# A two-layer decoder on one core: a fourth buffer for negated scores, half of the tails' sum and some elementwise work on Pool, the diagonals' product in one piece, reciprocals early

## The chip, the core and the metric

The kernel runs on one core of a Trainium2 chip, in one launch. The core has five engines, each with its own instruction stream that is executed in order: PE (TensorE, matmuls and transposes), DVE (VectorE), ACT (ScalarE), POOL (GpSimd) and SP (SyncE, which issues nearly all DMAs here). They wait for each other through semaphores. The metric is the device time of one execution in microseconds (us); lower is better. A time given for a kernel is the median of its runs.

## The reference, cut to what matters

Eight sequences (B = 8) of S = 256 tokens and width D = 256, 16 heads of 16, all in float32. Six sublayers follow each other, each with a residual and a LayerNorm without weights:

```python
x = norm(x + recurrence(x))                       # layer 0: gated linear scan
x = norm(x + cross(x, ctx, mask, side_bias))      # 16-head attention over ctx
x = norm(x + ternary_linear(quant(norm_gb(x))))   # one scale over all of x
x = norm(x + self_attention(x, rel_k, rel_v))     # layer 1: relative positions, clipped at 20
x = norm(x + cross(x, ctx, mask))                 # 16-head attention over ctx
x = norm(x + down(silu(gate(x)) * up(x)))         # hidden width 768
```

In the self-attention a score gets `q . rel_k[clip(j - i, -20, 20) + 20]` added, and the output gets `sum_j p[i, j] * rel_v[clip(j - i, -20, 20) + 20]`: 39 diagonals near the main one have a vector each, and all that lies further left or further right (the two tails) shares one vector a side. The quantisation scale of the ternary layer is a maximum over all eight sequences, so layer 1 can start for none of them before layer 0 is done for all.

## The kernel before, in words

**An order written out by a planner.** The kernel is generated by a small list scheduler (`Order`). Every piece of work is a Python generator that yields operations: `do(engine, cost, ready, emit)` for one engine, `either(ready, way, way)` where two engines could do it, `dma(...)` for SP. The planner holds a time at which each engine is free, and repeatedly takes the operation that can start first by its own cost figures (ties within 0.1 us go to the smaller urgency number, then to the earlier end), emits its instructions, and moves that engine's time on. So the order of every engine's stream is fixed when the program is built, and the costs in the source (`0.66`, `1.7`) are the planner's beliefs, not times of the chip. `copy` (L289 to L293) is such an `either` between DVE and ACT; it takes every transposed block of probabilities out of PSUM.

**Buffers are slots.** `get(slots, ...)` or a `Held` waits in the plan until a slot is free. PSUM has 8 banks. A quad of four heads takes four at once, each transposed block one, each attention item one for its output `pv` from its first `values` to the multiplication at L1041.

**An attention item** is one sequence in one of the three attentions (24 items). It projects q, k and v, then runs four quads (NS = 4) of four heads:
- `quad` (L896): the scores on PE (L913); for each head a DVE instruction pair at L941 that adds the bias, mask or band, negates, and takes the row minimum; its result `sn` is one of three `s_bufs` (L268), each held until ACT has read it.
- `head` (L952): two ACT exponentials (L957) which also sum the rows; four PE transposes of p (L502) and a copy to SBUF (L291 on DVE, L292 on ACT).
- `values` (L980): sixteen PE instructions at L995 that add into `pv`.
- `attend_out` (L1015), started after the last `values`: a reciprocal of the row sums on DVE (L1020), spread over 512 columns by POOL (L1026), transposed by PE, copied into `oT`, multiplied with `pv` (L1041), projected (L1056), added to x plus its bias row (L1049 on POOL, L1061 on DVE) and normalised.

**Self-attention has more.** The band of relative scores goes through DRAM by DMA and comes back skewed. After each quad, `tails_task` (L1377) sends p's diagonals to DRAM, masks the two tails with two POOL instructions (L1401, L1406: each 4 heads by 108 columns) and sums them with one DVE reduction over 864 elements (L1417). After each second quad two DMAs (L1425) bring the 39 diagonals into `acc`. `by_distance` (L1443), called by `attend_out`, then takes four rounds (two halves c by two blocks of tokens t), one after the other: four transposes of `acc` (L1455), a copy into one of two `at_bufs`, eight PE instructions at L1468 that add the product with `drv` into `pv`.

**A normalisation** (`norm`, L527) is statistics on DVE, the root on POOL (L543, L548), and a subtract-and-multiply on DVE (L553, two instructions of 256 columns; two pairs after the first cross-attention, which makes two normalised results).

**Other lines that the change touches.** L374 and L378 issue the first loads in the order bias columns, x of sequence 0, three weights. L1137 and L1585 turn a mask into 0 or a large negative number, on DVE. L1712 is the low half of a hidden activation (`sg - h`), on DVE, 24 times. `rows` (L407) holds bias rows for the whole kernel; `w0` is a pool of buffers that is given up when layer 0 is done.

Of the kernel before, what the change touches and what calls it, by code (L numbers as in the profile page):

```python
# [19 lines left out]
P = 128  # L20
# [202 lines left out]
def kernel(  # L223
# [43 lines left out]
    pts_bufs = slots(work, "pts", 8, [P, NQ, S])  # L267
    s_bufs = slots(work, "s", 3, [P, NQ, S])  # L268
    q_bufs = slots(work, "q", 3, [P, KC, S])
# [97 lines left out]
    def loads():  # L367
# [5 lines left out]

        t = yield from dma([0.0], 18432, lambda: nc.sync.dma_start(out=cols, in_=cols_in))  # L374
        yield from load_xT(0)
        for i in range(3):
            events["wa", i] = yield from dma(
                [0.0], 262144, lambda: nc.sync.dma_start(out=wa[i], in_=chunked(a_w[i]))  # L378
            )
        for b in range(1, 4):  # L380
            yield from load_xT(b)
        for a in range(3):
            pool = w0 if a == 0 else wts
            for i in range(2):
# [21 lines left out]
                )  # L406
                rows[o] = const.tile([P, D], F32, tag=f"rows{o}", name=f"rows{o}")  # L407
                events["rows", o] = yield from dma(
# [118 lines left out]
    def norm(y, t_y, make, name, make2=None):  # L527
# [21 lines left out]

        def scaled(make, i):  # L550
            dst = make()
            for t in range(NQ):
                nc.vector.tensor_scalar(  # L553
                    dst[:, t, :], y[:, t, :], mv[:, t, 0:1], rstd[:, i, t : t + 1], ALU.subtract,
                    ALU.mult,
                )

        t = yield from do("DVE", 0.9, [t_y], stats)
        t_r = yield from do("POOL", 0.9 if n == 1 else 1.1, [t], root)
        if n == 2:  # L560
            t_2 = yield from do("DVE", 0.66, [t_r], lambda: scaled(make2, 1))
        t = yield from do("DVE", 0.66, [t_r], lambda: scaled(make, 0))
        return t if n == 1 else (t, t_2)
# [388 lines left out]
    def head(it, n, j, p, s, nm, t, left, times):  # L952
# [165 lines left out]
    def item_x0(b):  # L1118
# [3 lines left out]
        if b > 1:  # L1122
# [134 lines left out]
    def layer1_self():  # L1257
        rel = layer1s.enter_context(tc.tile_pool(name="rel", bufs=1))
        kr_bufs = slots(rel, "kr", 2, [P, KC, 2, S - BW])
        wide_bufs = slots(rel, "wide", 2, [P, HH, PBW])  # L1260
        acc_bufs = slots(rel, "acc", 2, [P, KC, NQ, HH, NA])
        tail_bufs = slots(rel, "tail", 1, [P, NQ, 4, P - MR])
        at_bufs = slots(rel, "at", 2, [P, 4, P])
# [22 lines left out]
    def item_s1(b, kr_bufs, wide_bufs, acc_bufs, tail_bufs, at_bufs, band_bufs):  # L1286
# [90 lines left out]
        def tails_task(n, p, left, t_p):  # L1377
# [37 lines left out]
            t = yield from do(  # L1415
                "DVE", 1.0, [t],
                lambda: nc.vector.tensor_reduce(acc[:, c, :, own, 1], tail.tile, AX.X, ALU.add),  # L1417
            )
            tail.drop(t)
            it.t_tail.append(t)  # L1420
            if len(it.t_pb) in (2, 4) and n % 2 == 1:
                for g in range(P // BLK):
# [19 lines left out]

        def by_distance(t_pv):  # L1443
            for c in range(KC):
                t_a = yield from event(it.key("acc", c))
                for n in (2 * c, 2 * c + 1):
                    t_t = yield from event(it.key("tail", n))
                    t_a = max(t_a, t_t)
                for t in range(NQ):
                    ps = Held(banks, f"psa{b}_{t}_{c}")  # L1450
                    turned = lambda: ps.tile.rearrange("p a (j q) -> p (a j) q", q=P)

                    def emit():
                        for j in range(4):
                            nc.tensor.transpose(  # L1455
                                turned()[: 2 * NA, j, :],
                                it.acc.tile[:, c, t, 2 * j : 2 * j + 2, :].rearrange("p h r -> p (h r)"),
                                ident,
                            )

                    t_t = yield from do("PE", TURNS, [t_a, ps], emit)
                    at = yield from get(at_bufs, f"at{b}_{t}_{c}", t_t)
                    t_t = yield from copy([t_t, at.at], at.tile[: 2 * NA], turned()[: 2 * NA])
                    ps.drop(t_t)

                    def emit():
                        for j in range(4):
                            nc.tensor.matmul(  # L1468
                                it.pv.tile[32 * j : 32 * j + 32, c, t * P : (t + 1) * P],
                                drv[:, t, :],  # L1470
                                at.tile[: 2 * NA, j, :],
                                start=False,
                                stop=(t == NQ - 1 and c == KC - 1),
                                tile_position=(0, 32 * j),
                                skip_group_check=True,
                            )

                    t_pv = yield from do("PE", on_pe(256), [t_t, t_pv], emit, "v")
                    at.drop(t_pv)
            it.acc.drop(t_pv)  # L1480
            return t_pv

        it.by_distance = by_distance

# [83 lines left out]
    def item_x1(b):  # L1568
# [3 lines left out]
        if b > 0:  # L1572
# [84 lines left out]
    def gated(b, gu, dn, t_w, hT_bufs):  # L1657
# [13 lines left out]
        for i in range(NH // 2):  # L1671
            psg = Held(banks, f"fg{b}_{i}")

            def emit(ps, w):
# [34 lines left out]
            )  # L1709
            t = yield from do(  # L1710
                "DVE", on_dve(512), [t],
                lambda: nc.vector.tensor_tensor(h[:, 1], sg.tile, h[:, 0], ALU.subtract),  # L1712
            )
# [134 lines left out]
```

## Time and profile before

| | us |
|---|---|
| median of 3 runs (817.36 to 820.14) | 819.33 |
| the profiled execution | 817.66 |
| its span, first to last instruction | 815.9 |
| layer 0's recurrence and start, about | 0 to 75 |
| first cross-attention, about | 75 to 275 |
| ternary layer, then the first self-attention items alone | 275 to 380 |
| self- and cross-attention items in turn | 380 to 700 |
| feed-forward, with the last cross-attention items | 700 to 816 |

The stages overlap, so their borders are only where most of the work changes. The busy time of an engine is the time in which it had at least one instruction under way. PE's instructions are pipelined: the recorded duration of one is its latency, and the next one begins before it has ended. The granted PE clock was 0.995 of full speed over the span. What bounds the kernel is read from the lines that the prediction shows.

### The profile page before, as it was taken

To read this page: it belongs to the slowest core of one execution; us is meant where nothing else is said; L and a number is where in the kernel's file an instruction comes from. 1 tells how busy PE (TensorE), PEld (TensorE's weight loads), DVE (VectorE), ACT (ScalarE), POOL (GpSimd) and SP (SyncE) were. 2 spreads that over 40 slices of the span, in tenths; PEclk is the share of its full clock that TensorE was granted. 3 is DMA by queue.
4 is the path that set the end of the run, shared out by engine and by line. 5 is a ranking of instruction groups with operands and counts; after the bars stand their busy time and mean duration, and the time that the engine had idled before them with its cause. 6 is when DMAs were issued, how large, how long until landed. Compare 5 with 4: busy or idle time off the path is not lost.

```text
span 815.9 us, 21213 instructions
## 1 busy us (share of the span) xinstructions
PE 782.6 (96%) x7175; PEld 598.8 (73%) x7175; DVE 700.7 (86%) x2452; ACT 635.4 (78%) x2047; POOL 209.9 (26%) x398
## 2 busy tenths in 40 slices
PE   7999999999999999999999999999999999999995
PEld 6886777776777786656666777776777766799884
DVE  3899889988888698787899799899898998989985
ACT  2349988989988458896789799899899898846841
POOL 3520221121211044234333213242243322110020
PEclk9999999999999999999999999999999999999997
DMA  5735521100100449899976406645357443000001
GB/s 181 224 114 84 70 46 44 39 16 27 41 27 28 155 101 216 165 170 185 173 158 137 112 26 133 133 93 120 88 112 155 108 100 100 19 28 14 15 14 39
DMA packets 177681, 77.67 MB, mean 95 GB/s; under 512 B 155046, under 2 KB 171430, under 8 KB 177574
## 3 DMA queue, kind: packets, MB, share of 16 engines
q1 hardware_dynamic: 177574, 76.32, 41.9%
q8 instruction: 57, 0.93, 0.5%
q14 instruction: 50, 0.41, 0.2%
HBM read 41.66 MB, written 34.64 MB: 94 GB/s over the span
## 4 chain that ended last, share of the span: by engine, by line
PE 62%; DVE 13%; ACT 10%; DMA 6%; issue 4%; POOL 2%; SPq 2%; POOLq 0%; DVEq 0%; ACTq 0%
PE pt L502 14%; PE s L913 9%; PE pv L995 8%; ACT p L957 7%; PE pso L519 4%; DVE sn L941 4%; PE psv L519 4%; PE psq L508 4%; PE psk L508 3%; PE psd L1723 3%; ACT pts L292 2%; PE psa L1455 2%; DMA sk<-w 1%; PE fg L1678 1%; PE psr L1308 1%
## 5 line engine op out<-in xcount | busy, mean ns | idle before, releaser
L957 ACT ACTIVATE p<-sn,nm 128x256 f32<-128x256 f32 x768 | 381.3, 507 | 23.9 <-DVE nm L941 18.4
L502 PE MATMUL pt<-ident,p 128*128 128x128 f32 x1536 | 207.1, 277 | 5.2 <-ACT p L957 2.1
L502 PEld LDWEIGHTS pt<-ident,p 128*128 128x128 f32 x1536 | 169.4, 140 | 47.3 <-ACT p L957 24.7
L292 ACT COPY pts<-pt 128x512 f32<-128x512 f32 x274 | 147.7, 586 | 20.7 <-PE pt L502 19.8
L957 ACT ACTIVATION_READ_ACCUMULATOR p<-sn,nm 128x1 f32 x768 | 151.6, 197 | 0.0
L913 PE MATMUL s<-k,q 32*128 32x256 f32 (+2 forms) x1792 | 122.2, 371 | 2.6 <-DVE nm L941 1.2
L995 PE MATMUL pv<-pts,v 128*32 128x256 f32 x1536 | 107.4, 385 | 0.6 <-ACT pts L292 0.5
L941 DVE CUSTOM_DVE_ANT_0 sn<-s,band 128x256 f32<-128x256 f32 x256 | 93.9, 417 | 14.1 <-ACT p L957 6.3
L941 DVE CUSTOM_DVE_ANT_0 sn<-s,bias 128x256 f32<-128x256 f32 x256 | 93.8, 418 | 12.6 <-PE s L913 7.1
L941 DVE CUSTOM_DVE_ANT_0 sn<-s,hide 128x256 f32<-128x256 f32 x256 | 93.2, 417 | 12.9 <-PE s L913 10.6
L913 PEld LDWEIGHTS s<-k,q 32*128 32x128 f32 x1792 | 78.5, 184 | 34.2 <-issue 21.5
L291 DVE COPY pts<-pt 128x512 f32<-128x512 f32 x110 | 73.9, 683 | 4.5 <-PE pt L502 3.5
L995 PEld LDWEIGHTS pv<-pts,v 128*32 128x32 f32 x1536 | 42.9, 109 | 43.9 <-issue 19.8
L941 DVE DVE_READ_ACCUMULATOR2_ANT nm<- 128x1 f32 x768 | 62.8, 82 | 0.0
L519 PE MATMUL pso<-wvo,oT 128*128 128x256 f32 x192 | 47.1, 388 | 1.5 <-DVE oT L1041 1.5
L1026 POOL COPY rsw<-rsum 128x512 f32<-128x512 f32 x24 | 14.6, 610 | 126.2 <-DVE rsum L1020 99.0
L519 PEld LDWEIGHTS pso<-wvo,oT 128*128 128x128 f32 x192 | 34.8, 190 | 11.1 <-issue 3.2
L1318 POOL COPY w<-w 128x504 f32<-128x504 f32 x32 | 19.3, 603 | 87.8 <-DVE w L291 47.2
L1417 DVE TENSOR_REDUCE acc<-tail 128x8 f32<-128x864 f32 x32 | 33.4, 1043 | 3.0 <-POOL tail L1406 3.0
L1345 POOL COPY band<-ends 64x256 f32<-64x256 f32 x64 | 21.4, 360 | 47.1 <-DVE nm L941 47.0
L519 PE MATMUL psv<-wvo,ctxT 128*128 128x256 f32 x128 | 30.5, 381 | 0.3 <-DVE xnT L1093 0.3
L508 PE MATMUL psk<-ctxT,wqk 128*128 128x256 f32 x128 | 30.4, 381 | 0.0
(197 smaller groups left out, 1310.2 us busy)
## 6 DMA issues: line engine op xcount, KB each, us to landing
sk<-w SPq DMA_DIRECT2D x32, 416.0 KB
band<-sk SPq DMA_DIRECT2D x64, 104.0 KB
pb<-p SPq DMA_DIRECT2D x64, 104.0 KB
band<-sk SPq DMA_DIRECT2D x64, 84.0 KB
pb<-p SPq DMA_DIRECT2D x64, 84.0 KB
acc<-pb SPq DMA_DIRECT2D x32, 156.0 KB
ctxT<-in_ctxT SPq DMA_DIRECT2D x16, 256.0 KB
wpad<-in_qk_w SPq DMA_DIRECT2D x6, 512.0 KB
```

The lines of the kernel that those rows point to most:

```text
L291: ("DVE", on_dve(n), lambda: nc.vector.tensor_copy(dst, src)),
L292: ("ACT", on_act(n), lambda: nc.scalar.copy(dst, src)),
L502: nc.tensor.transpose(ps[:, c, t * P : (t + 1) * P], src[:, t, c * P : (c + 1) * P], ident)
L508: nc.tensor.matmul(ps, w[:, c, lo:hi], rhs[:, c, :], start=(c == 0), stop=(c == KC - 1))
L519: nc.tensor.matmul(ps[:, t, :], srcT[:, c, t * P : (t + 1) * P], w[:, c, :], start=(c == 0), stop=(c == KC - 1),)
L913: nc.tensor.matmul(ps[j].tile[:, t, first : first + w], it.q.tile[32 * j : 32 * j + 32, c, t * P : (t + 1) * P], k[32 * j : 32 * j + 32, c ...
L941: nc.vector.tensor_tensor_reduce(out=s.tile[:, t, :], in0=ps[j].tile[:, t, :], in1=tile[:, t, :], scale=-1.0, scalar=3e38, op0=ALU.add, op ...
L957: nc.scalar.activation(p.tile[:, j, q, :], s.tile[:, q, :], AF.Exp, bias=nm[:, q : q + 1], scale=-1.0, accum_out=it.sum_of(q, h),)
L995: nc.tensor.matmul(it.pv.tile[32 * j : 32 * j + 32, c, :], it.v.tile[:, k, head_of(n, j), :], pts.tile[:, k, :], start=(k == 0 and i == 0 ...
L1345: nc.gpsimd.tensor_copy(band.tile[0:BLK, :, t, lo:hi], it.ends[c][0:BLK, t, i:HH:2].unsqueeze(2).to_broadcast([BLK, 4, hi - lo]),)
L1417: lambda: nc.vector.tensor_reduce(acc[:, c, :, own, 1], tail.tile, AX.X, ALU.add),
L1723: nc.tensor.matmul(ps.tile[:, t, :], hT.tile[:, r, m, t * P : (t + 1) * P], dn[:, m, :], start=(m == 0 and r == 0), stop=(m == NH - 1 and ...
```

## The change

The list of what it does:
- `s_bufs` has four buffers instead of three. The bias rows of the first attention move from the pool that lasts for the whole kernel into `w0`.
- The first loads are issued in the order x of sequence 0, first weight, bias columns, other weights.
- In `norm`, the scaling of all but the recurrence's normalisation may run on DVE (planner's cost 0.66) or on POOL (1.7), whichever the planner finds free first.
- The low half at L1712 may run on DVE or on POOL (1.3).
- The two mask instructions (L1137, L1585) run on POOL.
- In `tails_task`, POOL adds the upper 54 columns of each masked tail to the lower 54, and the DVE reduction reads 432 elements instead of 864.
- The first part of `attend_out` (reciprocal, spreading, transposes, copy into `oT`) becomes a task of its own, `scales`, which starts when the last exponential's row sum is there, not after the last `values`.
- `by_distance` becomes `distances(c)`, a task that starts when the diagonals of the first half have been asked for; for each half it makes both blocks' transposes and copies, and then all sixteen PE instructions of the product in one piece, after the `values` of that half.

```diff
@@
-    s_bufs = slots(work, "s", 3, [P, NQ, S])
+    s_bufs = slots(work, "s", 4, [P, NQ, S])
@@ def loads():
-        t = yield from dma([0.0], 18432, lambda: nc.sync.dma_start(out=cols, in_=cols_in))
         yield from load_xT(0)
         for i in range(3):
             events["wa", i] = yield from dma(
                 [0.0], 262144, lambda: nc.sync.dma_start(out=wa[i], in_=chunked(a_w[i]))
             )
+            if i == 0:
+                yield from dma([0.0], 18432, lambda: nc.sync.dma_start(out=cols, in_=cols_in))
...
-                rows[o] = const.tile([P, D], F32, tag=f"rows{o}", name=f"rows{o}")
+                rows[o] = (w0 if a == 0 else const).tile([P, D], F32, tag=f"rows{o}", name=f"rows{o}")
@@ def norm(y, t_y, make, name, make2=None):
-        def scaled(make, i):
-            dst = make()
+        def scaled(engine, dst, i):
             for t in range(NQ):
-                nc.vector.tensor_scalar(
+                engine.tensor_scalar(
                     dst[:, t, :], y[:, t, :], mv[:, t, 0:1], rstd[:, i, t : t + 1], ALU.subtract,
                     ALU.mult,
                 )
+
+        def both(t, dst, i):
+            if name.startswith("l0a"):
+                return do("DVE", 0.66, [t], lambda: scaled(nc.vector, dst, i))
+            return either(
+                [t],
+                ("DVE", 0.66, lambda: scaled(nc.vector, dst, i)),
+                ("POOL", 1.7, lambda: scaled(nc.gpsimd, dst, i)),
+            )
...
-            t_2 = yield from do("DVE", 0.66, [t_r], lambda: scaled(make2, 1))
-        t = yield from do("DVE", 0.66, [t_r], lambda: scaled(make, 0))
+            t_2 = yield from both(t_r, make2(), 1)
+        t = yield from both(t_r, make(), 0)
@@ def head(it, n, j, p, s, nm, t, left, times):
         it.t_sums.append(t_e)
+        if len(it.t_sums) == H:
+            order.spawn(urgency(it, NS - 1), scales(it))
@@
-    def attend_out(it, t_pv):
-
-        ai, b = it.ai, it.b
+    def scales(it):
+
         rs = small.tile([P, NQ, H], F32, tag="rsum", name=f"rsum{it.name}")
...
-        oT = yield from get(oT_bufs, f"oT{it.name}", t)
+        oT = it.oT = yield from get(oT_bufs, f"oT{it.name}", t)
         t = yield from copy([t, oT.at], oT.tile, ps.tile)
         ps.drop(t)
+        events[it.key("scales")] = t
+
+    def attend_out(it, t_pv):
+
+        ai, b = it.ai, it.b
+        t = yield from event(it.key("scales"))
+        oT = it.oT
         if ai == 1:
-            t_pv = yield from it.by_distance(t_pv)
+            t_pv = yield from event(it.key("distances"))
@@ def item_x0(b):
-            "DVE", on_dve(512), [t_m, neg.at],
-            lambda: nc.vector.tensor_scalar(
+            "POOL", 0.6, [t_m, neg.at],
+            lambda: nc.gpsimd.tensor_scalar(
@@ def item_x1(b):
-            "DVE", on_dve(512), [t_m, hide.at],
-            lambda: nc.vector.tensor_scalar(
+            "POOL", 0.6, [t_m, hide.at],
+            lambda: nc.gpsimd.tensor_scalar(
@@ def tails_task(n, p, left, t_p):
+                for w in (54,):
+                    nc.gpsimd.tensor_tensor(
+                        tail.tile[:, :, :, 0:w], tail.tile[:, :, :, 0:w], tail.tile[:, :, :, w : 2 * w],
+                        ALU.add,
+                    )
+
-            t = yield from do("POOL", 1.06, [t_p, tail.at], emit)
+            t = yield from do("POOL", 2.1, [t_p, tail.at], emit)
...
-                "DVE", 1.0, [t],
-                lambda: nc.vector.tensor_reduce(acc[:, c, :, own, 1], tail.tile, AX.X, ALU.add),
+                "DVE", 0.55, [t],
+                lambda: nc.vector.tensor_reduce(
+                    acc[:, c, :, own, 1], tail.tile[:, :, :, 0:54], AX.X, ALU.add
+                ),
...
                 events[it.key("acc", c)] = t_d
+                if c == 0:
+                    order.spawn(urgency(it, NS - 1), distances(0))
@@
-        def by_distance(t_pv):
...
+        def distances(c):
+
+            t_a = yield from event(it.key("acc", c))
+            for n in (2 * c, 2 * c + 1):
+                t_t = yield from event(it.key("tail", n))
+                t_a = max(t_a, t_t)
+            at = yield from get(at_bufs, f"at{b}_{c}", t_a)
+            times = []
+            for t in range(NQ):
...
+                t_t = yield from do("PE", TURNS, [t_a, ps], emit)
+                t_t = yield from copy([t_t, at.at], at.tile[: 2 * NA, t], turned()[: 2 * NA])
+                ps.drop(t_t)
+                times.append(t_t)
+            t_v = yield from event(it.key("values", 2 * c + 1))
...
+            t_v = yield from do("PE", on_pe(512), [t_v, *times], emit, "v")
+            at.drop(t_v)
+            if c + 1 < KC:
+                yield from distances(c + 1)
+                return
+            it.acc.drop(t_v)
+            events[it.key("distances")] = t_v
@@ def gated(b, gu, dn, t_w, hT_bufs):
-            t = yield from do(
-                "DVE", on_dve(512), [t],
-                lambda: nc.vector.tensor_tensor(h[:, 1], sg.tile, h[:, 0], ALU.subtract),
+            t = yield from either(
+                [t],
+                ("DVE", on_dve(512), lambda: nc.vector.tensor_tensor(h[:, 1], sg.tile, h[:, 0], ALU.subtract)),
+                ("POOL", 1.3, lambda: nc.gpsimd.tensor_tensor(h[:, 1], sg.tile, h[:, 0], ALU.subtract)),
             )
```

More of the change, by code (lines that the diff above doesn't have):

```diff
@@ L1262, in layer1_self @@
         tail_bufs = slots(rel, "tail", 1, [P, NQ, 4, P - MR])
-        at_bufs = slots(rel, "at", 2, [P, 4, P])
+        at_bufs = slots(rel, "at", 1, [P, NQ, 4, P])
         bands = []
@@ L1441, in item_s1 @@
         it.t_pb = []
-        def by_distance(t_pv):
[L1444 to L1448, printed above, removed]
-                for t in range(NQ):
[L1450 to L1481, printed above, removed]
@@ L1483, in item_s1, with emit @@
-        it.by_distance = by_distance
+        def distances(c):
[6 more added lines that the diff above has]
+            for t in range(NQ):
+                ps = Held(banks, f"psa{b}_{t}_{c}")
+                turned = lambda: ps.tile.rearrange("p a (j q) -> p (a j) q", q=P)
+                def emit():
+                    for j in range(4):
+                        nc.tensor.transpose(
+                            turned()[: 2 * NA, j, :],
+                            it.acc.tile[:, c, t, 2 * j : 2 * j + 2, :].rearrange("p h r -> p (h r)"),
+                            ident,
+                        )
+                t_t = yield from do("PE", TURNS, [t_a, ps], emit)
[3 more added lines that the diff above has]
+            t_v = yield from event(it.key("values", 2 * c + 1))
+            def emit():
+                for t in range(NQ):
+                    for j in range(4):
+                        nc.tensor.matmul(
+                            it.pv.tile[32 * j : 32 * j + 32, c, t * P : (t + 1) * P],
+                            drv[:, t, :],
+                            at.tile[: 2 * NA, t, j, :],
+                            start=False,
+                            stop=(t == NQ - 1 and c == KC - 1),
+                            tile_position=(0, 32 * j),
+                            skip_group_check=True,
+                        )
+            t_v = yield from do("PE", on_pe(512), [t_v, *times], emit, "v")
[5 more added lines that the diff above has]
+            events[it.key("distances")] = t_v
```

## The prediction, made before the change was run

> **What bounds the kernel now.** I begin with the first part of the page and with the windows by stage (columns: length, then busy us of PE, its weight loads, DVE, ACT and POOL, clock, DMA share, GB/s).
>
> ```profile
> PE 782.6 (96%) x7175; PEld 598.8 (73%) x7175; DVE 700.7 (86%) x2452; ACT 635.4 (78%) x2047; POOL 209.9 (26%) x398
> ```
>
> ```profile
> 200.00:250.00 50.00, 49.56 (x470) 37.23 (x467) 43.95 (x179) 44.89 (x157) 9.06 (x12) 1.00 0.09 28
> 350.00:400.00 50.00, 47.15 (x463) 32.36 (x461) 39.71 (x139) 37.51 (x122) 19.38 (x42) 1.00 0.92 182
> 600.00:650.00 50.00, 49.62 (x521) 36.95 (x522) 44.38 (x172) 47.33 (x163) 15.92 (x33) 1.00 0.61 133
> 700.00:750.00 50.00, 49.81 (x434) 46.05 (x432) 44.16 (x105) 28.06 (x70) 5.42 (x10) 1.00 0.04 13
> ```
>
> PE looks full. If it were, no more than 815.9 - 782.6 = 33 us could be won. The Trainium skill (Trainium Kernel Development and Optimization, section Performance Expectations) says that matmul busy time is a bad measure because matmuls are pipelined, and names weight-load busy time instead: 73%. So I count PE's content from the timeline (start, length, what, how many):
>
> ```profile
> 524.21 1.89 PE L519 MATMUL psv<-wvo,xT_l0f 128*128 128x256 f32 x8
> 526.27 1.05 PE L995 MATMUL pv<-pts,v 128*32 128x256 f32 x16
> 530.15 2.78 PE L502 MATMUL pt<-ident,p 128*128 128x128 f32 x24
> ```
>
> One transpose is 277 ns long (its group's mean), but they follow each other by (2.78 - 0.28) / 23 = 0.109 us; a 256-column matmul by (1.89 - 0.38) / 7 = 0.216; a block of 16 counts between 0.67 (last start) and 1.05, I take 0.86. 1952 transposes 213 us, 960 projections 207, 192 blocks 165, feed-forward 576 x 0.12 (48 psd in 5.75 on the chain) 69, the rest about 29: 683 us, 84% of the span. By the row 33 us are open, by the skill's rule and this count some 130. DVE and ACT are as loaded: 44 and 45 of 50 us at 200, 44 and 47 at 600. **In the attention stages three engines share the bound**, and ACT and DVE are one pool of work, since `copy` takes either. At 350 all three are low beside DMA at 0.92: latency sets the pace. At 700 PE's weight loads fill 46 of 50: PE alone.
>
> **The change, part by part.**
>
> ```profile
> L1417 DVE TENSOR_REDUCE acc<-tail 128x8 f32<-128x864 f32 x32 | 33.4, 1043 | 3.0 <-POOL tail L1406 3.0
> L1712 DVE TENSOR_TENSOR hT<-sg,hT 128x512 fp32r<-128x512 f32 x24 | 16.6, 694 | 3.4 <-ACT hT L1708 2.8
> L553 DVE TENSOR_SCALAR x_l1x<-xb,mv_l1x,rs_l1x 128x256 f32<-128x256 f32 x16 | 8.5, 573 | 0.0
> L553 DVE TENSOR_SCALAR x_l0x<-xb,mv_l0x,rs_l0x 128x256 f32<-128x256 f32 x16 | 5.8, 406 | 0.0
> L683 POOL TENSOR_SCALAR a<-z 128x512 f32<-128x512 f32 x8 | 5.3, 666 | 12.1 <-ACT z L674 11.4 <-DVE h L705 0.7
> L1049 POOL TENSOR_TENSOR xb<-x_l0f,rows 128x512 f32<-128x512 f32 x8 | 10.2, 1272 | 0.0
> ```
>
> *Off DVE.* Tails: a reduction of 512 took 679 ns (L1109), of 864 1043, so 432 takes about 596: 32 x 0.447 = 14.3 us. Masks: 3.3 (L1137) + 4.4 (L1585) = 7.7. Scaling: the six rows that may move sum to 41.2 us; the planner gives them to POOL when DVE is not free at once, DVE is 86% busy, I take 70%: 29. Low half: 16.6, I take 60%: 10. Sum 61 busy us. About 100 instructions go, and consecutive DVE instructions overlap by some 0.08 us, so DVE gains 61 - 8 = 53 us of issue time.
>
> *Onto POOL.* Tail sums: L1049's 1272 for 512 columns, less the fixed 191 (L543, two columns), scaled to 432: 1.10 us, x32 = 35. Masks 16 x 0.62 = 10. Low halves 14 x 1.28 = 18. Scaling is in no row of POOL: from below, 191 + (618 - 191) / 2 = 0.40 for 256 columns by L683's undisturbed 618, 0.81 a pair; from above the planner's 1.7. I take 0.81, the nearest row: 34 pairs, 27 us (58). POOL goes from 210 to about 300 (331), 37 to 41%: hidden as throughput. As latency, a pair costs 0.16 to 1.05 us more than on DVE, plus a wait behind what POOL's in-order queue holds (roots, tails, the band's filling and the widening at L1318); I count 0.3 us for it.
>
> *A rule that speaks against it.* The skill (SBUF — State Buffer, section Who interferes with whom) says that a DVE instruction in a two-port mode, or with two SBUF inputs, and a POOL instruction lock each other out wholly; with one SBUF input there is no contention. The trace shows both: x_l1x at 573 against 406 is DVE behind POOL (at 696.56 a pair took 1.94 us while POOL's 1.47 us cast ran), while sn at L941, from PSUM and one SBUF tile, has the same 417 in all three stages. If every added POOL us blocked DVE, the 90 us would eat the 53. But the DVE work that can be locked out is small after the change: the remaining scaling 12, low halves 7, k (L1595) 7, quantisation 8, gates 12, about 46 us. With POOL's share 11 points higher, that is about 46 x 0.11 = 5 us of added blocking; against it the scaling's present excess over 406 ns, about 6 us, mostly leaves with it. I count zero, ends -5 and +5.
>
> *What 53 us are worth.* Shared with ACT: 53 / (700.7 + 635.4) = 4.0%. It counts where these two set the pace, 60 to 300 and 400 to 700, 540 us: 21 us. PE's content and the chains between engines hold some of it back; I take 60%: **13 us**.
>
> *Fourth buffer.* Waits: the first number is the total.
>
> ```profile
> DVE sn L941 <- ACT p L957: 13.6, 28, 1.3
> ```
>
> With four buffers a whole quad's negations run ahead and give their PSUM banks back. These 13.6 us are DVE idle time; what comes next (the bank, ACT) is late by nearly as much: **2 us**, ends 0 and 7.
>
> *Product in one piece.* The chain of a self-attention item (start, length, what):
>
> ```profile
> 422.17 4.22 DMA acc<-pb
> 426.38 0.14 issue
> 426.52 0.61 PE psa L1455 x4
> ...
> 430.30 0.58 PE psa L1455 x4
> ...
> 430.91 0.59 ACT at L292
> 431.50 0.04 issue
> 431.54 0.42 PE pv L1468 x8
> ```
>
> The half after the last diagonals keeps its DMA, transposes, copy and product; it loses one round, 0.6 + 0.6 + 0.4 plus hand-overs, 2 us, and the first half, which now runs earlier. That lies open for the two items of the latency-bound stretch at most: **3 us** (0 to 8). No DMA moves; `oT` and `acc` are held no longer than before, PSUM `pv` shorter.
>
> *Reciprocals early.* 0.35 + 0.61 + 0.60 + 0.59 and hand-overs leave the end of each item. For the last cross-attention, `pv` was ready at 777.56 and multiplied at 781.08. Other work hides it in 23 items; **1 us** (0 to 3). The new task's work stands ahead of the last copies of p, which costs nothing when DVE gained more.
>
> *First loads.* x of sequence 0 goes out 0.46 us earlier (1.25 to 0.79), as does the weight PE waits for at 4.97; the columns land later, but ACT needs them at 8.76 and they were in use from 2.61: **0.5 us**. The bias rows' new place costs no instruction.
>
> Sum 13 + 2 + 3 + 1 + 0.5 = 19.5. 817.7 - 19.5 = 798.2 for the profiled execution; the median of before stands 1.7 above it, so **800 us**.
>
> **Rivals.** About 0.3%, 2.5 us, is what can be told from no change.
> 1. *DVE and ACT set the pace everywhere in the attention, and the plan uses all of it*: 21 instead of 13, the buffer and the product at their better halves, +9: 783 to 791, say **787**. For it: ACT 47 of 50 at 600. Against: PE's 84%.
> 2. *The offload doesn't happen*: the planner rarely picks POOL at 1.7 against 0.66, only tails and masks move. Relief 22, worth 5: 819.3 - 11 = **808**.
> 3. *PE is the bound after all*: the gain is latency only. **816**. Against: the count of 683.
> 4. *POOL's queue becomes the late link* (slower). The root and the scaling are consecutive on POOL, behind tails that hold it for 2.2 us instead of 1.1. At 1.7 a pair, each normalisation is later by 1.05 + 0.3. It decides once more than 19.5 / 1.35 = 14 of the 40 scaled normalisations lie open; at 20, 819.3 - 19.5 + 27 = **827**. For it: the items' chain runs through normalisation into the next item's projections. Against: items are interleaved, and POOL waits now, not DVE on it (DVE xn behind the root: 4.0 us in 8).
>
> **From the cases to the numbers.** Forecast (792 to 809, rival 2 included) 0.58; full relief 0.20; hidden 0.10, of which half is beyond 0.3%; slower 0.12. The range 784 to 818 leaves out the slower case and a little of the full one. Faster 0.82, same 0.06, slower 0.12.
>
> **What would show it.** DVE busy near 640, POOL near 300, ACT lower or equal by copies moving to DVE; L1417 near 596 ns; L553 with POOL rows near 400 ns for 256 columns; the wait of sn for ACT mostly gone; the windows of 200 and 600 with PE's instruction count up by 2 to 3%. If POOL's scaling takes 850 ns and DVE or PE waits for it in tens of us, rival 4 holds; if DVE falls and the counts per window don't rise, rival 3.

## The result, and the profile after

| | before | after |
|---|---|---|
| median of six runs each on one chip, us | 819.14 (817.36 to 821.86) | 825.06 (823.38 to 825.76) |
| ratio, 95% interval | 1 | 1.0064 [1.0045, 1.0083] |
| span of the profiled execution, us | 815.9 | 824.0 |
| where the planner's own costs put the end, us | 802.9 | 790.5 |
| span minus that: the **lag** of the chip behind its plan, us | 13.0 | 33.6 |

The change makes the kernel slower by 0.64%. The last two rows, worked out from the program that generates the kernel, are the shortest account of it: by its own beliefs the planner wins 12.4 us, the chip falls behind the plan by 20.6 us more, and the difference, 8.2, is the loss between these two executions (824.0 - 815.9 = 8.1). The profiled execution of after is the slowest of its six; between the medians the loss is 5.9 us.

First part of the page, and the windows by stage (columns as before: length, PE, weight loads, DVE, ACT, POOL, clock, DMA share, GB/s):

```profile
PE 779.1 (95%) x7175; PEld 598.2 (73%) x7175; DVE 671.8 (82%) x2391; ACT 620.7 (75%) x2008; POOL 365.6 (44%) x520
```

```profile
200.00:250.00 50.00, 48.06 (x455) 35.18 (x456) 44.16 (x171) 41.11 (x144) 14.85 (x16) 1.00 0.08 22
350.00:400.00 50.00, 47.70 (x484) 34.51 (x483) 37.20 (x130) 39.49 (x129) 27.92 (x49) 1.00 0.90 166
600.00:650.00 50.00, 49.33 (x554) 37.65 (x553) 43.88 (x182) 48.48 (x165) 27.61 (x42) 1.00 0.59 119
700.00:750.00 50.00, 50.00 (x454) 44.85 (x453) 41.21 (x112) 33.11 (x93) 19.04 (x21) 1.00 0.08 27
```

DVE and ACT were relieved by 43.6 us of busy time together; POOL took 155.7 more. At 200, PE started 455 instructions instead of 470, and ACT's work fell from 44.89 to 41.11: as if less reached these engines. At 350 and 600 the counts are higher than before, by 5% and 6%. The last normalisation of the first cross-attention ended at 280.3 (before 275.0), the last of the ternary layer at 321.3 (310.7), the last of the second cross-attention at 796.6 (788.1). So after is 10.7 us late at 321, and from there to the end 2.6 of them are won back.

Groups of instructions (busy us, mean ns of one; then the engine's idle time before them and what ended it):

```profile
L1440 DVE TENSOR_REDUCE acc<-tail 128x8 f32<-128x432 f32 x32 | 19.0, 593 | 7.1 <-POOL tail L1429 7.0
L1429 POOL TENSOR_TENSOR tail<-tail 128x432 f32<-128x432 f32 x32 | 30.9, 965 | 2.7
L553 POOL TENSOR_SCALAR x_l0f<-yf,mv_l0f,rs_l0f 128x256 f32<-128x256 f32 x14 | 17.5, 1254 | 0.7
L553 DVE TENSOR_SCALAR x_l1f<-yf,mv_l1f,rs_l1f 128x256 f32<-128x256 f32 x4 | 1.5, 410 | 2.2 <-POOL rs_l1f L549 2.2
L1154 POOL TENSOR_SCALAR neg<-mask 128x512 f32<-128x512 int32 x8 | 15.5, 1939 | 0.7
L1618 POOL TENSOR_SCALAR hide<-mask 128x512 f32<-128x512 uint8 x8 | 15.7, 1963 | 17.2 <-DMA mask<-in_mask 12.0 <-DVE nm L950 4.8
L1746 POOL TENSOR_TENSOR hT<-sg,hT 128x512 fp32r<-128x512 f32 x8 | 10.5, 1315 | 20.2 <-ACT hT L1741 20.2
```

Two prices differ from the plan's. A scaling of 256 columns takes 1254 ns on POOL and 410 on DVE, so a pair is 2.5 us where the plan wrote 1.7. A mask takes 1.94 us where the plan wrote 0.6. The six groups of scaling on POOL hold 66 instructions and 83.5 us: 33 of the 48 pairs that may move did.

The chain of waits in the ternary stage of after (start, length, what), and then the same stage of before:

```profile
290.27 0.20 POOL rs_l0f L544
290.47 0.07 issue
290.55 0.72 POOL rs_l0f L549
291.26 0.09 issue
291.36 2.52 POOL x_l0f L553 x2
293.87 0.08 issue
293.96 0.25 POOL rs_l0f L544
294.21 0.07 issue
294.28 0.97 POOL rs_l0f L549
```

```profile
297.33 0.65 DVE x_l0f L553 x2
297.98 0.66 DVE st_l0f L538 x2
298.64 0.22 DVE mv_l0f L540 x2
298.86 0.64 DVE yf L1233
...
300.35 0.65 DVE x_l0f L553 x2
```

Here POOL's queue is the chain: root, scaling, root, scaling. The first sequence takes 3.7 us (293.96 - 290.27), the next two on this chain 4.1 and 4.6. Before, DVE's queue was the chain, at 3.0 us a sequence (300.35 - 297.33). Waits for what POOL scaled (total, times, longest) stand ahead of PE as well:

```profile
PEld ps_xn L503 <- POOL xn L553: 6.2, 7, 1.1
PEld ps_l0f L503 <- POOL x_l0f L553: 4.4, 4, 1.6
DVE yf L1250 <- POOL x_l0f L553: 3.7, 5, 1.4
PEld ps_l1a L503 <- POOL x_l1a L553: 3.4, 5, 1.1
```

14 us of waiting of PE's weight loads hang on these three tiles; before, ps_xn behind DVE's scaling was 2.3.

The plan shows where the lag begins. In it, this last ternary normalisation ends at 303.3 before and at 298.6 after; on the chip it ended at 310.65 (309.93 + 0.72) and 321.34 (318.91 + 2.43):

```profile
309.93 0.72 DVE L553 TENSOR_SCALAR x_l0f<-yf,mv_l0f,rs_l0f 128x256 f32<-128x256 f32 x2
```

```profile
318.91 2.43 POOL L553 TENSOR_SCALAR x_l0f<-yf,mv_l0f,rs_l0f 128x256 f32<-128x256 f32 x2
```

So at the end of layer 0 the chip is already 22.7 us behind the plan, where before it was 7.3. 16.7 of the 22.7 (before 6.6 of the 7.3) were there at the end of the first cross-attention.

### The profile page after: what moved, and what is told of

The parts are those of the page before. It is cut to its first block, busy times and chain, and to the rows that moved or that the text cites. A ratio compares the mean times of both kernels' runs of the same rounds, so it can differ in the third digit from the quotient of the medians.

```text
span 824.0 us, 21293 instructions
## 1 busy us (share of the span) xinstructions
PE 779.1 (95%) x7175; PEld 598.2 (73%) x7175; DVE 671.8 (82%) x2391; ACT 620.7 (75%) x2008; POOL 365.6 (44%) x520
## 4 chain that ended last, share of the span: by engine, by line
PE 66%; ACT 10%; DVE 9%; POOL 7%; DMA 3%; issue 3%; SPq 0%; POOLq 0%; DVEq 0%; ACTq 0%
PE pt L503 15%; PE s L922 9%; PE pv L1006 8%; ACT p L966 7%; PE psk L509 4%; PE psq L509 3%; DVE sn L950 3%; PE psv L520 3%; PE pso L520 3%; PE psd L1757 3%; PE psz L509 2%; ACT pts L292 2%; POOL xn L553 2%; PE psr L1325 2%; PE psh L509 2%
## 5 line engine op out<-in xcount | busy, mean ns | idle before, releaser
L966 ACT ACTIVATE p<-sn,nm 128x256 f32<-128x256 f32 x768 | 381.0, 506 | 20.5 <-DVE nm L950 14.1
L503 PE MATMUL pt<-ident,p 128*128 128x128 f32 x1536 | 210.3, 278 | 5.9 <-ACT p L966 2.8
L503 PEld LDWEIGHTS pt<-ident,p 128*128 128x128 f32 x1536 | 169.4, 140 | 52.9 <-ACT p L966 30.6
L292 ACT COPY pts<-pt 128x512 f32<-128x512 f32 x264 | 143.5, 588 | 36.8 <-PE pt L503 34.8
L922 PE MATMUL s<-k,q 32*128 32x256 f32 (+2 forms) x1792 | 114.8, 369 | 0.1
L1006 PE MATMUL pv<-pts,v 128*32 128x256 f32 x1536 | 105.6, 385 | 1.4 <-DVE nm L950 0.7
L950 DVE CUSTOM_DVE_ANT_0 sn<-s,hide 128x256 f32<-128x256 f32 x256 | 93.0, 419 | 10.7 <-PE s L922 5.3
L922 PEld LDWEIGHTS s<-k,q 32*128 32x128 f32 x1792 | 74.4, 184 | 28.0 <-issue 16.4
L291 DVE COPY pts<-pt 128x512 f32<-128x512 f32 x120 | 80.7, 685 | 13.0 <-PE pt L503 11.4
L1036 POOL COPY rsw<-rsum 128x512 f32<-128x512 f32 x24 | 14.6, 610 | 92.4 <-DVE rsum L1030 57.9
L1741 ACT CAST hT<-sg 128x512 fp32r<-128x512 f32 x24 | 14.8, 622 | 25.0 <-DVE sg L1736 23.2
L1429 POOL TENSOR_TENSOR tail<-tail 128x432 f32<-128x432 f32 x32 | 30.9, 965 | 2.7
L1362 POOL COPY band<-ends 64x256 f32<-64x256 f32 x64 | 21.5, 362 | 22.2 <-DVE nm L950 22.0
```

The lines of the kernel that those rows point to most:

```text
L291: ("DVE", on_dve(n), lambda: nc.vector.tensor_copy(dst, src)),
L292: ("ACT", on_act(n), lambda: nc.scalar.copy(dst, src)),
L503: nc.tensor.transpose(ps[:, c, t * P : (t + 1) * P], src[:, t, c * P : (c + 1) * P], ident)
L922: nc.tensor.matmul(ps[j].tile[:, t, first : first + w], it.q.tile[32 * j : 32 * j + 32, c, t * P : (t + 1) * P], k[32 * j : 32 * j + 32, c ...
L950: nc.vector.tensor_tensor_reduce(out=s.tile[:, t, :], in0=ps[j].tile[:, t, :], in1=tile[:, t, :], scale=-1.0, scalar=3e38, op0=ALU.add, op ...
L966: nc.scalar.activation(p.tile[:, j, q, :], s.tile[:, q, :], AF.Exp, bias=nm[:, q : q + 1], scale=-1.0, accum_out=it.sum_of(q, h),)
```

## The experiments

They ran on several chips, whose times for the kernel before lie between 825.5 and 828.2 us, so only ratios to the kernel before on the same chip are compared, with 95% intervals.

**First set: take back the two suspected moves, one by one, and tell the planner true prices.** r1 puts all scaling back on DVE, r2 the masks, r3 both; r4 leaves all moves and corrects the costs.

```diff
 def both(t, dst, i):                              # r1, r3
-    if name.startswith("l0a"):
+    if True:
...
-    "POOL", 0.6, [t_m, neg.at],                   # r2, r3; the same for hide
-    lambda: nc.gpsimd.tensor_scalar(
+    "DVE", on_dve(512), [t_m, neg.at],
+    lambda: nc.vector.tensor_scalar(
...
-    ("POOL", 1.7, lambda: scaled(nc.gpsimd, dst, i)),   # r4
+    ("POOL", 2.5, lambda: scaled(nc.gpsimd, dst, i)),
...
-    "POOL", 0.6, [t_m, neg.at],                   # r4; the same for hide
+    "POOL", 1.95, [t_m, neg.at],
```

> The changed kernel with all normalisations' scaling on DVE again. Theory A (POOL's scaling, 2.45 us a pair instead of the 0.81 I took, lies open where the normalisations follow each other, in the ternary stage and behind the last first-cross-attention item): the 33 POOL pairs go, DVE gets some 21 us of issue time back, the ternary stage loses its 5 us, and the whole is near 813 us (809 to 818). Theory B (the regrouping of reciprocals and diagonals, or a worse order by the planner's luck, is what costs): 823 us or more, since DVE only gets more work. Theory C (POOL is only late, DVE's relief is what counts): 830.

> The changed kernel with the sixteen mask instructions on DVE again. On POOL they took 1.95 us each where the plan has 0.6, so POOL runs 1.35 us behind the plan after each. Theory A (slow POOL instructions hold up what is behind them in its queue): 820 us (817 to 823), most of it in the first cross-attention. Theory B: 825, no difference beyond 0.3%.

> The changed kernel with both scaling and masks on DVE again; tail sums, low halves, fourth buffer, early reciprocals and the regrouped product stay. Theory A: faster than before the change, near 808 us (803 to 814), since what is left of the offload is POOL work at its planned price. Theory B: 824 or more, as the regrouping is still in it.

> The changed kernel with the planner told POOL's measured costs: 2.5 for a pair of scalings, 1.95 for a mask. Theory A in its form 'the plan believed a wrong price': the planner still gives POOL some pairs, but not where they lie open, 812 us (807 to 818). In its form 'these instructions are too dear wherever they run': 818 to 823. Theory B: 825.

Measured: r1 1.0030 [1.0013, 1.0048], r2 1.0097 [1.0067, 1.0127], r3 0.9992 [0.9973, 1.0011], r4 1.0045 [1.0024, 1.0066]. With both moves back the loss is gone, but so is any gain: the rest of the change shows none. And r2 stands above after, though work left the slow engine; their intervals overlap. If that is more than noise, either the masks were better on POOL, or each build shuffles the order and the shuffle itself has a price.

r4 missed its 812 us, yet it says most about the cause. With true prices the planner still gives POOL 27 pairs of scalings: eight in the first cross-attention, as in after, and three instead of seven in the ternary layer. But the chip no longer falls behind so far in layer 0. At the end of the first cross-attention its lag is 7.5 us (after 16.7), at the last ternary normalisation 9.0, against 22.7 in after, 21.5 in r2 (scaling on POOL), 10.0 in r1 (masks on POOL) and 10.4 in r3, each in its one profiled execution. In the second deals of the fourth set below it is 17.9 with scaling alone on POOL and 11.9 with masks alone. So the lag of layer 0 came with the false price of the scaling. Yet r4's plan ends at 798.3, r3's at 797.3: at true prices the two moves bring the plan nothing, and r4's time shows no gain either. Later in the kernel single profiled executions scatter too much for this comparison.

**Second set: the other parts alone on the kernel before, and a control.** b4 changes no work at all: it only widens the planner's tie window, so that other operations are taken first.

```diff
-    s_bufs = slots(work, "s", 3, [P, NQ, S])      # b1, with the bias rows in w0
+    s_bufs = slots(work, "s", 4, [P, NQ, S])
...
-    t = yield from do("POOL", 1.06, [t_p, tail.at], emit)   # b3, with the sum of 54 columns
+    t = yield from do("POOL", 2.1, [t_p, tail.at], emit)
...
-WINDOW = 0.1                                      # b4
+WINDOW = 0.12
```

b2 takes only the new tasks `scales` and `distances` from the change's diff.

> The kernel before with the fourth buffer for negated scores alone (and the bias rows' new place, which makes room for it). My step: -2 us (0 to -7), ratio 0.991 to 1.000. Theory B (the regrouping of reciprocals and diagonals costs): this one is 1.000 or below. Theory D (nearly any edit re-deals the plan, and the kernel before is a good deal among them): up to 1.01 although the edit only gives room.

> The kernel before with the early reciprocals and the diagonals' product in one piece alone. My step: -4 us, ratio 0.995. Theory B: slower by 7 us or more, ratio 1.008 or more, with the loss of PE content between 380 and 450 us. Theory A (only POOL's dear instructions cost): 0.995 to 1.000. Theory D: anything from 0.995 to 1.010, with the loss not tied to the product or the reciprocals.

> The kernel before with the tails half summed by POOL alone: 0.965 us more on POOL and 0.447 us less on DVE, 32 times, at the price the plan has. DVE gains 14 us; by my step 'a quarter of what DVE gains comes out as time' 3.5 us, ratio 0.996. Theory A: 0.995 to 0.999. Theory B: 0.995 to 0.999. Theory D: 0.995 to 1.010.

> A control: the kernel before with one number of the planner changed that touches no work (ties within 0.12 us instead of 0.1). Theories A and B: the same time, ratio 0.998 to 1.002. Theory D: a difference of 3 us or more, rather slower than faster, since the numbers of the order by hand were chosen with the plan of before.

Measured: b1 1.0055 [1.0034, 1.0075], b2 1.0035 [1.001, 1.006], b3 1.005 [1.003, 1.007], **b4 1.0028 [1.0013, 1.0044]**. I had not expected every part to be slower, and the control gives a reason: another order of the same instructions costs 0.28%, and its interval overlaps those of all three parts. The kernel before is a good deal of its planner. No part's worth can be read from one build. Their plans end at 800.0 (b1), 807.3 (b2) and 802.2 (b3) against 802.9 before, so b2's loss was in its plan already, while b1 and b3 lost on the chip. In b1, the waits of `sn` show what the fourth buffer met:

```profile
DVE sn L941 <- PE s L913: 22.6, 22, 5.2
DVE sn L941 <- ACT p L957: 10.3, 20, 1.4
```

The wait for ACT fell by 3.3 us from 13.6, and the wait for the scores rose by 2.7 from 19.9.

**Third set: the same order with cheaper instructions, and more deals.** c1 keeps every instruction's place in after, but lets POOL do the same arithmetic in another form: the mask by an add and a multiplication (masks hold only 0 and 1), the scaling as y·rstd - mean·rstd with the product made by one small instruction more per result. c2 is r3, c3 after and c4 before, each with another tie window (0.12, 0.12, 0.15).

```diff
-    neg.tile, mask.tile, 0.0, NEG_INF, ALU.is_equal, ALU.mult
+    neg.tile, mask.tile, -1.0, -NEG_INF, ALU.add, ALU.mult
...
+    nc.gpsimd.tensor_tensor(shift[:, i], mv[:, :, 0], rstd[:, i], ALU.mult)
...
-    dst[:, t, :], y[:, t, :], mv[:, t, 0:1], rstd[:, i, t : t + 1], ALU.subtract,
-    ALU.mult,
+    dst[:, t, :], y[:, t, :], rstd[:, i, t : t + 1], shift[:, i, t : t + 1], ALU.mult,
+    ALU.subtract,
```

> The changed kernel in its own order on every engine, with two forms of POOL instruction exchanged: a mask is (mask - 1) * 1e30 (add, multiply) instead of (mask == 0) * -1e30 (compare, multiply), and POOL's scaling is y * r - m * r (multiply, subtract, with m * r from one more small POOL instruction after the root) instead of (y - m) * r. Measures the disputed prices by themselves. If the form makes the price, a mask takes about 0.62 us (as L683's multiply-add) and a pair of scalings 0.8 to 1.2, below the plan's 1.7; then theory A expects the lag of the plan in layer 0 and the ternary stage (15 us) to go and the kernel to be at 0.985 to 0.995 of before. If a [128, 1] operand makes the price, the pair stays near 2.4 us and only the masks' part goes: 1.003 to 1.006. Theory D alone (order, not prices): 1.004 to 1.008.

> The changed kernel with scaling and masks on DVE (as r3_both_dve, 0.999) and ties within 0.12 us: a second deal of that kernel, whose own plan ends at 787.5 instead of 797.3. Theory D (each deal differs by some tenths of a per cent, and what an edit is worth is seen only over several deals): between 0.985 and 1.003. If plans carry over to the chip one to one: 0.987.

> A second deal of the changed kernel (ties within 0.12 us), whose plan ends at 789.7 as against 790.5. Theory A: again slower than before, 1.003 to 1.010, as the dear POOL instructions are in it. Theory D alone: anywhere from 0.99 to 1.01.

> A third deal of the kernel before (ties within 0.15 us; 0.12 gave 1.003). Theory D (the kernel before is a good deal of its own): 1.001 to 1.010. Otherwise 0.997 or less.

Measured: c1 1.0167 [1.0126, 1.0207], **c2 0.9833 [0.9802, 0.9865]**, c3 1.0082 [1.0057, 1.0106], c4 1.0053 [1.0035, 1.0072]. c1 was a miss that taught something. Its groups:

```profile
L563 POOL TENSOR_SCALAR x_l0f<-yf,rs_l0f,sh_l0f 128x256 f32<-128x256 f32 x14 | 17.4, 1248 | 0.7
L1164 POOL TENSOR_SCALAR neg<-mask 128x512 f32<-128x512 int32 x8 | 5.0, 620 | 0.7
L1260 DVE SCALAR_TENSOR_TENSOR yf<-psf,deq,x_l0x 128x512 f32<-128x512 f32 x8 | 6.0, 751 | 8.6 <-POOL x_l0f L563 7.4 <-PE psf L520 1.0 <-issue 0.3
```

The mask became three times cheaper, the scaling did not: its price is not in the order of its arithmetic (both forms subtract, and both read two columns). POOL's masks lost 21 us of work, the roots gained 11.7 us of small instructions ahead of each scaling, and the kernel lost another 1.0%. DVE's wait for x_l0f went from 3.7 to 7.4 us. c1 has after's order, so no new deal is in this 1.0%: what is added to the normalisation's chain on POOL comes out as time. That the masks' own length hardly matters is only suggested here, since both were changed at once.

c2 beats both kernels. It has all of the change except the two moves. Its first line and windows:

```profile
PE 776.3 (96%) x7175; PEld 599.1 (74%) x7175; DVE 682.5 (84%) x2443; ACT 635.6 (78%) x2040; POOL 253.7 (31%) x438
```

```profile
200.00:250.00 50.00, 49.08 (x489) 36.61 (x488) 44.41 (x184) 47.89 (x162) 7.79 (x11) 1.00 0.07 23
350.00:400.00 50.00, 44.56 (x424) 31.37 (x423) 33.61 (x121) 33.47 (x108) 24.14 (x47) 0.97 1.04 166
600.00:650.00 50.00, 49.88 (x556) 37.17 (x558) 46.05 (x186) 49.70 (x172) 20.09 (x34) 1.00 0.52 102
```

At 200 PE starts 489 instructions (before 470, after 455) and ACT works 47.89 of 50: the picture that I had forecast for after. At 350 it starts fewer than before: its gain is made in the attention stages and partly given back where DMA is at 1.04.

**Fourth set: more deals, and one move at a time.** d1 is r3 and d2 after, with window 0.15; d3 is r2 (scaling on POOL, masks on DVE) and d4 is r1 (masks on POOL), with 0.12.

```diff
-WINDOW = 0.1
+WINDOW = 0.15      # d1, d2; 0.12 in d3, d4
```

> A third deal (ties within 0.15 us) of the changed kernel with scaling and masks on DVE; the kernel before stands at 1.0053 with these ties. Theory A (the rest of the change is worth 1% over deals; POOL's dear instructions spoil it): 0.985 to 1.000. Theory D alone: 0.995 to 1.010, no better than before over the three deals.

> A third deal of the changed kernel whole. Theory A: 1.000 to 1.012, and at least 0.5% above d1. Theory D alone: no fixed sign against d1.

> Second deal (ties within 0.12 us), scaling on POOL or DVE as in the change, masks on DVE. From the first square scaling costs 0.7% and masks nothing: 0.990 to 1.010, clearly over c2's 0.983. If the masks are what costs: 0.983 to 0.988.

> Second deal, masks on POOL at their real 1.95 us, scaling on DVE. If scaling is what costs: 0.981 to 0.992. If the masks are: 0.995 to 1.010.

Measured: d1 0.9901 [0.9868, 0.9934], d2 1.0145 [1.0121, 1.0169], d3 0.9985 [0.9969, 1.0002], d4 1.0018 [1.0005, 1.0032]. Now the deals can be compared. "End of plan" and "lag" stand in the order of the windows; the lag is the ratio times 815.9 us, less the end of the plan (for after that gives 30.6, where its one profiled span gave 33.6):

| version | ratio at 0.10 / 0.12 / 0.15 | mean | end of plan, us | lag, us |
|---|---|---|---|---|
| before | 1 / 1.0028 / 1.0053 | 1.0027 | 802.9 / 805.8 / 804.7 | 13.0 / 12.4 / 15.5 |
| change without the two moves (r3, c2, d1) | 0.9992 / 0.9833 / 0.9901 | 0.9909 | 797.3 / 787.5 / 796.8 | 17.9 / 14.8 / 11.0 |
| masks alone on POOL (r1, d4) | 1.0030 / 1.0018 | 1.0024 | 793.9 / 796.4 | 24.4 / 21.0 |
| scaling alone on POOL (r2, d3) | 1.0097 / 0.9985 | 1.0041 | 795.4 / 794.2 | 28.4 / 20.5 |
| after (both; c3, d2) | 1.0064 / 1.0082 / 1.0145 | 1.0097 | 790.5 / 789.7 / 800.3 | 30.6 / 32.9 / 27.4 |

Three things come out of it. First, the change without the two moves is below before in the three pairs by 0.08, 1.95 and 1.52 points, the first of them within its interval: 1.2 in the mean of three deals that scatter by 1.6, and already in the plan (804.5 to 793.9 in the means), with a lag as before (13.6, 14.6). Second, the two moves cost 0.72, 2.49 and 2.44 points: 1.9 in the mean. They bring the plan nothing (793.9 to 793.5) and double the lag (14.6 to 30.3), and the lags of the two versions do not overlap. Third, single ratios scatter by a point and more with the deal alone, so one build settles nothing here.

The granted clock does not explain this. Over the span its median in c2's runs was 0.9895 and in d2's 0.9905, against 0.9925 and 0.991 for the kernel before on the same chips, and c2 is faster than before, d2 slower. In r4 (0.984, before 0.993) and in e1 below (0.985, before 0.9935) a lower clock may be a part of the loss; that was not separated.

For the scaling, the four comparisons with the rest equal are all losses: after against r1 +0.34, r2 against r3 +1.05, c3 against d4 +0.64, d3 against c2 +1.52. For the masks they are -0.33, +0.38, +0.97 and +1.85: three losses of four. The lag is longer in all eight comparisons.

**Fifth set: are the masks dear by their price?** e1 is r1 with the mask in its cheap form and its true cost in the plan; e2 is the same with window 0.12.

```diff
-    "POOL", 0.6, [t_m, neg.at],
+    "POOL", 0.63, [t_m, neg.at],                  # 0.66 for hide
...
-    neg.tile, mask.tile, 0.0, NEG_INF, ALU.is_equal, ALU.mult
+    neg.tile, mask.tile, -1.0, -NEG_INF, ALU.add, ALU.mult
```

> Ties within 0.1 us; masks on POOL as (mask - 1) * 1e30, planned at their real 0.63 and 0.66 us; scaling on DVE. If the dear form was the cost: at or below r3's 0.9992, 0.990 to 1.000. If the move itself was: 1.002 or more, as r1.

> The same with ties within 0.12 us; its plan ends at 800.1, c2's at 787.5. If the dear form was the cost: below d4's 1.0018, 0.983 to 0.998 (the plan's own end lets it stand above c2). If the move itself was: 1.000 or more.

Measured: e1 1.0085 [1.0058, 1.0112], e2 1.0105 [1.0077, 1.0133]; lags 25.6 and 24.4. Both missed: a mask at a third of the price, known to the planner, is no better than the dear one (r1 1.0030, d4 1.0018). So its price is not what makes it a loss. What all builds with masks on POOL share is a wait; the group in e1, and the same group in c2, where it is DVE's:

```profile
L1618 POOL TENSOR_SCALAR hide<-mask 128x512 f32<-128x512 uint8 x8 | 4.9, 618 | 21.1 <-DMA mask<-in_mask 20.8
```

```profile
L1618 DVE TENSOR_SCALAR hide<-mask 128x512 f32<-128x512 uint8 x8 | 3.9, 487 | 0.7 <-DMA mask<-in_mask 0.7
```

POOL comes to the mask before its DMA has landed and stands still for 20.8 us in all, here and in the other builds with masks on POOL between 12.0 and 29.7; DVE, with more to do ahead of it, stands for 0.7. What was queued behind it is in d2's POOL timeline (bracket: idle time before, and what ended it):

```profile
601.23 1.94 POOL L1618 TENSOR_SCALAR hide<-mask 128x512 f32<-128x512 uint8 x1 [5.39 <-DMA mask<-in_mask]
603.25 0.19 POOL L544 TENSOR_SCALAR rs_l1a<-mv_l1a 128x2 f32<-128x2 f32 x1
603.53 0.72 POOL L549 TENSOR_TENSOR rs_l1a<-rs_l1a,half 128x2 f32<-128x2 f32 x1
```

A root follows the mask at once. But its input was there only at 602.83, so of 7.3 us of mask and waiting this one lost 0.4. That the waits together make the masks' lag is thus a reading of the traces, not shown; no run moved the masks' DMA ahead.

## Why the prediction was wrong

**Price of a scaling on POOL: the step that failed.** I took 0.81 us a pair "by the nearest row", L683, with 1.7 as the upper end. It measured 2.5: both ends were too low. So a pair is 1.9 us longer than on DVE, where I had 0.16 to 1.05, and the plan built on 1.7 fell behind in layer 0: by 22.7 us instead of 7.3, and by only 9.0 once the planner had the true price (r4). L683 has two constants as operands; the scaling has two columns of 128 values. That these columns make the price fits c1, but is not shown, since no run had a form without the subtraction. The share that moves, 70%, was right (33 of 48).

**What it does to the chain.** Rival 4, POOL's queue as the late link, had the right mechanism, and I gave it 0.12. My reason against it, that POOL waits for others and not they for it, was read from a trace in which POOL did, of each normalisation, only the root. In the ternary stage seven of the eight scalings run through this queue. Rival 4's sum (827 against 825.06 measured) is right only by accident: of the 19.5 us that it kept, r3 shows none at this deal.

**Masks.** 0.62 us was taken from the same L683; it measured 1.94 to 1.96. But e1 and e2 show that the price isn't the point; I had not asked what the mask waits for, and what stands behind it in an in-order queue.

**POOL's added work** was 155.7 us instead of 90, outside the upper end too. Single terms: tail sums 30.9 (35), low halves 10.5 (18, with 8 of 24 moved instead of 14), masks 31 (10), scaling 83 (27).

**Relief of DVE.** 61 busy us went off DVE by my list; it shows 28.9. Scaling left as priced (28.3 us, priced 29), but only 4.4 us of the low halves (priced 10). And work that may run on either engine moved from ACT to DVE: the copies at L291 grew from 108.8 to 119.2 us, ten copies of probabilities among them. Together DVE and ACT lost 43.6. I had said DVE at about 640; it is 671.8.

**What relief is worth: 13 us.** Not refuted, but not measured by itself. Without the two moves my own terms are 13 x 24 / 61 = 5.1 for tails and low halves and 6.5 for the small steps, 11.6 together; over three deals it gains 10 us in the mean, and no run parts these terms. At the deal that was measured, r3 gains 0.7 us.

**The missing term: the order.** The sum had no term for re-dealing a plan that fits well. The control has no other work than before and loses 0.28%, c4 0.53%. With it, the forecast would have moved 2 to 4 us towards no change. And the plan itself could have been asked: by its own prices, the false ones included, the change wins 12.4 us, less than my sum of 19.5.

**Small steps.** Fourth buffer, 2 us: in b1 most of the wait for ACT that went came back as waiting for the scores, as the prediction said; in after the wait rose to 15.8. Its time (1.0055) can't be told from a deal. Product in one piece and early reciprocals, 4 us: b2 against the control shows no gain (1.0035, 1.0028). First loads, 0.5: no run told it apart. Contention, taken as zero: the scaling left on DVE took 474 ns in the mean (471 before), the low halves left there 761 (694), 1 us in all; larger blocking does not show in these rows.

**What stays open:** what exactly the masks cost on POOL; and why r3 at window 0.10 shows nearly nothing of c2's gain. Of the 13.0 us between them, 9.8 lie between their plans (797.3 and 787.5); 3.1 are lag. Against before, r3 loses in the stretch where DMA sets the pace (length, PE, weight loads, DVE, ACT, POOL, clock, DMA share, GB/s; before, then r3):

```profile
380.00:420.00 40.00, 37.95 (x389) 27.32 (x388) 36.97 (x134) 32.51 (x110) 16.86 (x36) 1.00 0.90 169
```

```profile
380.00:420.00 40.00, 33.96 (x299) 23.55 (x298) 28.01 (x109) 24.89 (x84) 17.59 (x35) 0.91 1.03 160
```

299 PE instructions instead of 389 in these 40 us, with DMA at 1.03; r3's lag grew by 10.9 us from the end of the ternary layer to the third self-attention item, where before's shrank by 0.7 (about 1.4 of it is the slower chip: 1% of that stretch of 140 us). c2 falls behind by 8.3 there too, so this parts both from before, not r3 from c2. The planner's model of DMA times is the suspect; no run tried another one.

## What to carry to other kernels

Before work is moved to an idle engine, price it by a row with the same operands, not only the same operation, and ask what stands ahead of it and behind it in that engine's queue: an engine with 26% of busy time became the chain of the ternary stage when most of the scaling passed through it. Where an order is generated by a planner, compare versions over several deals, with a control that changes only the order, and read the gap between the plan and the chip: where a plan gets better while its lag doubles, tell it the true times first. Here that took the lag out of layer 0, and the plan's gain with it (r4); e1 and e2 lagged at true mask prices as well, so it is not the only cause of lag.

## What the hardware showed that was not expected

- POOL's time for a `tensor_scalar` differed by form. With two constants, multiply and add, 128x512 took 712 ns in the mean (L692); add and multiply on a mask 618 to 660; compare and multiply on the same mask 1937 to 1982 over the builds; with two operands of 128x1, subtract and multiply (after) or multiply and subtract (c1) alike, 1225 to 1309 for 128x256, so more than three times as long per column as the first. DVE took 414 for the compare and multiply and 405 to 410 for the two columns where it was undisturbed.
- The granted clock fell below 1.00 in some stretches with few PE instructions, 0.91 in r3's 380 to 420 (299) and 0.97 in c2's 350 to 400 (424), against 1.00 in before (389 and 463). But it stayed at 1.00 in after's 380 to 420 with 344, so the count alone does not decide it.
